# Moving sixteen checks of a matrix from one stage of a four-layer graph kernel to another

## The chip, the cores and the metric

The kernel runs on one core of a Trainium2 chip, in one launch. The metric is the device time of the launch in microseconds (us). Five engines have queues of their own: TensorE (PE, with its weight loads shown apart as PEld), VectorE (DVE), ScalarE (ACT), GpSimd (POOL) and SyncE (SP), the last of which here only issues transfers.

## The reference

Four layers of different graph networks share one node matrix `x` (4096 x 64) and one adjacency matrix `adj` (4096 x 4096, float32, entries 0 or 1). Each layer normalises `x`, computes its update and adds it.

```python
# layer 0: 8 attention heads over adj, then a second, single-headed attention on their output
mask = (adj > 0)[None]
...
e_o = jax.nn.leaky_relu(o1[:, None] + o2[None, :], ALPHA)
att_o = jax.nn.softmax(jnp.where(mask[0], e_o, NEG), axis=-1)
out = att_o @ Who
return jnp.tanh(out)
...
# layer 1: a weight and a distance for each pair of nodes
adj_att = jax.nn.sigmoid(left[:, None] + right[None, :] + b_att[0]) * adj
x_local = logmap(x[:, None, :], x[None, :, :], c)
support_t = jnp.einsum('ij,ijd->id', adj_att, x_local)
return proj(expmap(x, support_t, c), c)
...
# layer 2: mean of the neighbours, a dense layer, row norm
h_neigh = (adj @ X + X) / deg
...
# layer 3: the last 100 neighbours of a row, weighted by powers of one half
mask = (adj != 0).astype(support.dtype)
rank = jnp.cumsum(mask, axis=1)
...
w = mask * jnp.where(pos > 0, DECAY ** (k - pos), 0.0)
out = w @ support + bias
```

## The kernel before

The 4096 nodes are 32 blocks of 128 (`NB`), or 8 groups of 512 (`NG`). The adjacency matrix arrives transposed. It is turned once into bytes that are edge masks (0 or 56 as an integer, 0 or 1 as an 8-bit float) and written to DRAM as `mask_d`, one tile for each four blocks of sources (`q`, 8 of them) and half of the targets. All later stages read this mask and not the matrix.

That is only right if every value of the matrix is 0 or 1. So the kernel reads the whole float matrix a second time and checks it: `count_odd` (line 951) loads one 128 x 2048 piece (1 MB) into a tile `raw`, of which there are two, through SP's queue, and one DVE instruction (line 955) counts the elements for which "greater than 0" differs from the value itself. The count goes to one column of `bad`. There are 64 pieces; an iterator `todo` (line 959) hands out their numbers in order of the calls. At the end of the fast path (lines 2827 to 2830) the columns of `bad` are added on DVE, reduced over the partitions on GpSimd and compared with zero, and if anything was counted, the general kernel computes all again (line 2833). The calls of `count_odd` in the kernel before: sixteen in the output's attention (line 2105), and 48 beside the pairs of layer 1 (`check_edges`, line 2389).

The stages, one after another in the trace: the eight heads of layer 0 (to about 935 us), the output's attention with the node parts of layer 1 (to 1218), the pairs of layer 1 (to 1676), its closing and layer 2, and from about 1830 to 2030 the last layer.

*The output's attention* (lines 1957 to 2191). Four units `u` of 1024 targets each; a unit runs over eight blocks `q` of four source blocks. For each `q` SP loads a mask tile `mo` (three buffers); DVE makes its complement `nmo8`, which GpSimd's queue stores as `noedge_d` for layer 1; and for each pair of source blocks `split_edges` (line 1192) takes on ScalarE the sign of source score plus target score into `st` (line 1205), on DVE the products `B` (line 1211) and, for three pairs of four, `C` (line 1219). TensorE multiplies values with these products into `acco` (line 2132), and the factors of the denominators with `B` and `mo` into `ddo` (lines 2145, 2151). At a unit's end the sums are copied out (`evD`, `evB`, `evC`); `finish_unit` and the generator `layer1_nodes`, a long row of small DVE and ScalarE instructions, run within the next unit. The checks stand ahead of every other `q`. `behind(prepared.ins)` puts their DVE instruction behind the last one of the preparation.

*Layer 2 and the last layer* (`layers_fast`, line 2521). Layer 2 sums over the mask in two halves of the targets (tile `m`, line 2683) and closes each half with four calls of `layer2_group` (line 2628), each of which ends with the values of the last layer: `SS` and the remainder `lo` (line 2673). The last layer again has four units of 1024 targets and eight blocks `q` of mask tiles `m` (here called `m3`, line 2747, three buffers). For each of the 32 source blocks `j` TensorE computes the ranks into `pv` (lines 2754 and 2762), ScalarE turns them into weights `w` (`w3b`, line 2771), and TensorE adds the weighted values of the block before (`add_up`, line 2736) into two `sacc` banks. At a unit's end the sums are copied out to `ev` (line 2778), one by ScalarE and one by DVE, folded by TensorE (`pn3`), added to bias and `x` on DVE (`og`) and stored on GpSimd's queue (line 2793).

*Order.* The program is laid out by a scheduler that takes instructions by their place in the program as their inputs and buffers come free; each engine's queue then runs in that fixed order. A `with tc.issue_after(ins)` block adds one rule: instructions within it that run on the engine of `ins` come after `ins` there. Of a `count_odd` in such a block only the DVE instruction is bound if `ins` is on DVE; its load on SP's queue isn't. The pairs of layer 1 are in a block that keeps DVE, ScalarE and TensorE in the order of the program (`in_order`); the attention's units and the last layer are not.

Of the kernel before, what the change touches and what calls it, by code (L numbers as in the profile page):

```python
# [18 lines left out]
ALU = mybir.AluOpType  # L19
# [816 lines left out]
def kernel(  # L836
# [24 lines left out]
    nc = tc.nc  # L861
# [89 lines left out]
    def count_odd(pool, c):  # L951

        raw = pool.tile([P, HW], F32, name="raw", tag="raw", bufs=2)
        nc.sync.dma_start(raw, adjT[c % NB * P : (c % NB + 1) * P, c // NB * HW : (c // NB + 1) * HW])
        nc.vector.scalar_tensor_tensor(  # L955
            raw, raw, 0.0, raw, ALU.is_gt, ALU.not_equal, accum_out=bad[:, c : c + 1]
        )
# [83 lines left out]
    with ExitStack() as l0:  # L1041
# [134 lines left out]
        @contextmanager  # L1176
        def behind(*marks):

            with ExitStack() as e:
                for i in marks:  # L1180
                    e.enter_context(tc.issue_after(i))
                yield
# [726 lines left out]
        with ExitStack() as ob:  # L1909
# [185 lines left out]
            for u in range(4):  # L2095
                us = slice(u * HO2, (u + 1) * HO2)
                hs = slice((u % 2) * HO2, (u % 2 + 1) * HO2)
                accB, accC = (
                    [ps_acc.tile([P, G], F32, name="acco", tag="acc") for _ in range(NK)]
                    for _ in range(2)  # L2100
                )

                dd = ps_acc.tile([P, G], F32, name="ddo", tag="acc")
                for q in range(NQ):
                    if q % 2 == 0:
                        with behind(prepared.ins):
                            count_odd(work, next(todo))
                    m = work.tile([P, JT, HO2], U8, name="mo", tag="mo", bufs=3)
                    nc.sync.dma_start(m, mask_d[q][u // 2][:, :, hs])
                    nm8 = work.tile([P, JT, HO2], U8, name="nmo8", tag="nmo8")  # L2110
                    nc.vector.tensor_scalar(
                        nm8.bitcast(I32), m.bitcast(I32), EDGES4, None, ALU.bitwise_xor
                    )
                    nc.gpsimd.dma_start(noedge_d[q][u // 2][:, :, hs], nm8)
                    B2 = []
                    for t in range(0, JT, 2):
                        j0 = q * JT + t
                        edges = m[:, t : t + 2, :]
                        whole = j0 // 2 % 4 == 1
                        B, C = split_edges(  # L2120
                            work, srow[:, us], nto[:, j0 : j0 + 2], edges, j0, NB + 1, not whole, 4
                        )
                        B2.append(B)
                        products = [(accB, YB[:, j0 : j0 + 2], B), (accC, YC[:, j0 : j0 + 2], C)]
                        if whole:
                            products[1] = accC, YC[:, j0 : j0 + 2], edges.bitcast(F8)
                            yn = YCn[:, j0 // 8].rearrange("p i (s d) -> p i s d", d=D)
                            products.append((accC, yn, B))
                        for acc, Y, E in products:
                            for i in range(2):  # L2130
                                for k in range(NK):
                                    sums = nc.tensor.matmul(
                                        acc[k],
                                        lhsT=Y[:, i].rearrange("p s d -> p (s d)"),
                                        rhs=E[:, i, k * G : (k + 1) * G],
                                        start=j0 + i == 0,
                                        stop=acc is accB and j0 + i == NB - 1,
                                    )
                    with behind(sums.ins):
                        for t in range(JT):  # L2140
                            j = q * JT + t
                            fl = dict(start=(j == 0), stop=(j == NB - 1))
                            for k in range(NK):
                                ks = slice(k * G, (k + 1) * G)
                                nc.tensor.matmul(
                                    dd[k * O : (k + 1) * O, :],
                                    lhsT=YD1[:, j],
                                    rhs=B2[t // 2][:, t % 2, ks],
                                    **fl,
                                )  # L2150
                                nc.tensor.matmul(
                                    dd[(NK + k) * O : (NK + k + 1) * O, :],
                                    lhsT=YD2[:, j],
                                    rhs=m[:, t, ks].bitcast(F8),
                                    **fl,
                                )
                    if q == 0 and pending:
                        finish_unit(*pending)
                        beside = layer1_nodes(slice((u - 1) * OB, u * OB), work, aug)
                        pending = None  # L2160
                    elif u:
                        for _ in range(2):
                            next(beside, None)
                assert not u or next(beside, None) is None
                evD = work.tile([P, G], F32, name="evD", tag="evD", bufs=1)
                nc.vector.tensor_copy(evD, dd)
                em = work.tile([P, G], F16, name="emo", tag="emo", bufs=1)
                nc.vector.tensor_scalar(em, evD, 0.0, None, ALU.is_equal)
                evs = [evD]
                for k in range(NK):  # L2170
                    ev = work.tile([P, G], F32, name="evB", tag="evB", bufs=NK)
                    (nc.vector.tensor_copy if k else nc.scalar.copy)(ev, accB[k])
                    evs.append(ev)
                for k in range(NK):
                    nc.tensor.matmul(
                        accC[k],
                        lhsT=meano[NK * O :, k].rearrange("p s d -> p (s d)"),
                        rhs=em[NK * O :],
                        start=False,
                        stop=True,  # L2180
                    )
                    ev = work.tile([P, G], F32, name="evC", tag="evC", bufs=NK)
                    (nc.vector.tensor_copy if k else nc.scalar.copy)(ev, accC[k])
                    evs.append(ev)
                pending = (u, evs)
# [335 lines left out]
    def layers_fast(es, wide, *sums):  # L2521
# [41 lines left out]
            base=0,  # L2563
            channel_multiplier=1,
        )
        ready = []

# [58 lines left out]
        def layer2_group(b0, part, deg):  # L2628
# [41 lines left out]
                )  # L2670
            nc.scalar.copy(SS[:, bs, 0, :], pu)
            lo = work.tile([P, GB, D], F32, name="lo3", tag="lo3")
            nc.vector.tensor_tensor(lo, pu, SS[:, bs, 0, :], ALU.subtract)
            nc.scalar.activation(SS[:, bs, 1, :], lo, AF.Copy, scale=LO)


# [53 lines left out]
        for u in range(4):  # L2730
# [14 lines left out]
            for q in range(NQ):  # L2745
                m = work.tile([P, JT, HO2], U8, name="m3", tag="m3", bufs=3)
                nc.sync.dma_start(m, mask_d[q][u // 2][:, :, hs])
                for t in range(JT):
                    j = q * JT + t

                    pv = ps_v.tile([P, HO2], F32, name="pv", tag="pv")
                    for k in range(NK):
                        r = ((u % 2) * NK + k) * O
                        nc.tensor.matmul(  # L2754
                            pv[:, k * G : (k + 1) * G],
                            lhsT=blk[r : r + O, j, :],
                            rhs=late[r : r + O, u // 2, :],
                            start=True,
                            stop=False,
                        )  # L2760
                    for k in range(NK):
                        nc.tensor.matmul(  # L2762
                            pv[:, k * G : (k + 1) * G],
                            lhsT=tri,
                            rhs=m[:, t, k * G : (k + 1) * G].bitcast(F8),
                            start=False,
                            stop=True,
                        )

                    w = work.tile([P, HO2], I16, name="w3b", tag="w3b", bufs=3)  # L2770
                    nc.scalar.activation(w, pv, AF.Relu)  # L2771
                    if last is not None:
                        add_up(*last)
                    last = (j, w)
# [113 lines left out]
```

## Time and profile before

| what | value |
|---|---|
| median of 3 runs | 2041.64 us (2033.41 to 2043.93) |
| profiled execution | 2039.13 us |
| its span in the profile | 2037.1 us |
| granted TensorE clock over the span | 0.938 |
| PE busy | 1815.8 us (89%) |
| DVE busy | 1530.0 us (75%) |
| ACT busy | 1476.9 us (72%) |
| POOL busy | 83.3 us (4%) |
| one check on DVE (line 955), 64 of them | 2282 ns and 81 ns for its accumulator |
| its load, 1 MB, from issue to landing | 6.0 us (median) |

A table of windows gives, for stretches of the span, how long each engine was busy. A group line gives line, engine, operation, output and inputs, shapes and count, then after the bar the busy time, the mean of one in ns, and, after a second bar, how long the engine stood idle just before and what ended that. In a timeline line a bracket at the end says how long the engine had been idle and on whom it waited. TensorE's matmuls overlap each other, so the busy time of TensorE is an upper figure.

The page's slices (fortieths of the span, some 51 us each, digits are tenths) show the stages: DVE is busy to 7 to 9 tenths up to the 36th slice and idle in the last three, TensorE is busy nearly everywhere.

```profile
PE   5889989999999999996788958999999995789998
DVE  5779988998789879996989867888788788533000
ACT  2768987899689878993778847777777753227676
```

### The profile page before, as it was taken

The page shows a single profiled execution, that of the slowest core. Times are in us where ns is not written, and L with a number is a line of the kernel's source. Part 1 is how long each engine was busy: PE and PEld are TensorE (multiplying, and loading weights), DVE is VectorE, ACT ScalarE, POOL GpSimd, SP SyncE. Part 2 cuts the span into 40 slices and gives each one's busy share as a digit, 9 for nine tenths or more (in the row PEclk, how much of TensorE's full clock was granted, in tenths as well). Part 3 has the DMA queues.
Part 4 walks back from the last instruction along what each step waited for, and adds up shares of the span by engine and source line. Part 5 has one row for each costly group of instructions (what it writes and reads, how often), then busy time and mean ns, then how long its engine had stood idle before and what let it go on. Part 6 is the DMA issues. An engine that isn't in the chain of part 4 may idle for free. (4 is left out here: it accounts for less than half of the span.)

```text
span 2037.1 us, 44155 instructions
## 1 busy us (share of the span) xinstructions
PE 1815.8 (89%) x19323; PEld 821.8 (40%) x19340; DVE 1530.0 (75%) x2239; ACT 1476.9 (72%) x1439; POOL 83.3 (4%) x125
## 2 busy tenths in 40 slices
PE   5889989999999999996788958999999995789998
PEld 3444445444444444443234442333333333344332
DVE  5779988998789879996989867888788788533000
ACT  2768987899689878993778847777777753227676
POOL 2000100100000000001011100000000000000000
PEclk8899999999999999997899977999999996899999
DMA  9945555434211111103686406444344334412232
GB/s 112 178 115 99 100 99 72 164 118 172 86 49 49 48 49 54 54 2 125 254 276 227 163 17 235 137 145 143 124 140 140 124 134 151 152 63 70 91 99 64
DMA packets 117016, 239.05 MB, mean 117 GB/s; under 512 B 11062, under 2 KB 84006, under 8 KB 102054
## 3 DMA queue, kind: packets, MB, share of 16 engines
q1 hardware_dynamic: 101996, 192.95, 28.1%
q0 software_dynamic: 14816, 43.18, 11.8%
q8 instruction: 153, 2.51, 0.5%
q14 instruction: 51, 0.42, 0.1%
HBM read 245.37 MB, written 49.46 MB: 145 GB/s over the span
## 5 line engine op out<-in xcount | busy, mean ns | idle before, releaser
L1205 ACT ACTIVATE st<-srow,nt 128x2048 int8<-128x2048 f32 x352 | 682.8, 1994 | 78.9 <-DVE B L1211 78.1
L1211 DVE TENSOR_TENSOR B<-st,mres 128x1024 int32<-128x1024 int32 x256 | 311.7, 1220 | 70.5 <-PE accC L1541 46.6
L1541 PE MATMUL accB<-B,ybh 128*32 128x512 fp8e4 x3072 | 340.6, 384 | 13.3 <-DVE B L1211 13.3
L1541 PE MATMUL accD<-B,ybh 128*32 128x512 fp8e4 x2048 | 303.0, 388 | 23.0 <-DVE h L1657 23.0
L1541 PEld LDWEIGHTS <-ybh 128*32 128x32 bf16 (+1 forms) x6656 | 197.4, 98 | 236.8 <-issue 74.8
L1541 PE MATMUL accC<-mres,ych 128*32 128x512 fp8e4 x2272 | 269.2, 381 | 0.0
L1541 PE MATMUL accC<-B,ycn 128*32 128x512 fp8e4 x2272 | 269.0, 381 | 0.0
L1541 PE MATMUL accL<-B,ybh 128*32 128x512 fp8e4 x1536 | 221.6, 390 | 4.6 <-DVE h L1661 4.5
L1541 PEld LDWEIGHTS <-ych 128*32 128x32 f16 x4096 | 170.2, 99 | 116.1 <-issue 11.3
L1199 DVE TENSOR_SCALAR st<-srow,nt 128x2048 uint8<-128x2048 f32 x160 | 205.4, 1284 | 2.5
L2339 PE MATMUL accj<-sg,who 128*64 128x512 f32 (+1 forms) x512 | 197.8, 616 | 5.9 <-DVE sg L2332 5.5
L2339 PE MATMUL acci<-sg,who 128*64 128x512 f32 (+1 forms) x512 | 197.8, 616 | 0.0
L2295 ACT ACTIVATE yt<-pu,consts 128x512 f32<-128x512 f32 x144 | 98.7, 687 | 98.7 <-PE pu L2294 98.6
L2284 ACT ACTIVATE sg<-pl,rb 128x512 f32<-128x512 f32 x256 | 160.9, 679 | 8.2 <-PE pl L2279 5.2
L2771 ACT ACTIVATE w3b<-pv 128x1024 int16<-128x1024 f32 x128 | 131.0, 1024 | 42.4 <-PE pv L2762 41.2
L1205 ACT ACTIVATE st<-srowo,nto 128x1024 int8<-128x1024 f32 x128 | 138.3, 1138 | 25.0 <-DVE B L1211 24.9
L1541 PE MATMUL accC<-C,ych 128*32 128x512 fp8e4 x1824 | 149.3, 393 | 0.8 <-DVE C L1219 0.8
L955 DVE SCALAR_TENSOR_TENSOR raw<-raw 128x2048 f32<-128x2048 f32 x64 | 146.1, 2282 | 3.3 <-DMA raw<-in_adj_dram 3.3
L1219 DVE TENSOR_TENSOR C<-B,mres 128x1024 int32<-128x1024 int32 x114 | 139.5, 1225 | 3.6
L1541 PEld LDWEIGHTS <-ycn 128*32 128x32 f16 x2272 | 108.4, 97 | 62.7 <-issue 1.9
L2332 DVE SCALAR_TENSOR_TENSOR sg<-pf,sg 128x512 f32<-128x512 f32 x112 | 72.1, 685 | 38.9 <-PE pf L2329 38.9
L2778 DVE COPY ev<-sacc 128x512 f32<-128x512 f32 x4 | 2.8, 691 | 124.8 <-PE sacc L2736 124.8
(497 smaller groups left out, 2756.4 us busy)
## 6 DMA issues: line engine op xcount, KB each, us to landing
raw<-in_adj_dram SPq DMA_DIRECT2D x64, 1024.0 KB, 6.0
mo<-edges SPq DMA_DIRECT2D x32, 512.0 KB, 4.9
noedge<-nmo POOLq DMA_DIRECT2D x32, 512.0 KB, 4.3
nm<-noedge SPq DMA_DIRECT2D x64, 256.0 KB, 3.1
m<-edges SPq DMA_DIRECT2D x16, 1024.0 KB, 4.8
m<-edges SPq DMA_DIRECT2D x32, 512.0 KB, 3.8
srow<-srow_d SPq DMA_DIRECT2D x15, 1024.0 KB, 6.7
mres<-in_adj_dram POOLq DMA_DIRECT2D x8, 1024.0 KB, 35.4
```

Of the source, the lines that this page charges most:

```text
L955: nc.vector.scalar_tensor_tensor(raw, raw, 0.0, raw, ALU.is_gt, ALU.not_equal, accum_out=bad[:, c : c + 1])
L1199: nc.vector.tensor_scalar(st[:, i, :].bitcast(U8), srow, negs[:, i : i + 1], EDGE, ALU.is_gt, ALU.mult)
L1205: nc.scalar.activation(st[:, i, :], srow, AF.Sign, bias=negs[:, i : i + 1], scale=-1.0)
L1211: nc.vector.tensor_tensor(B.bitcast(I32), st.bitcast(I32), edges.bitcast(I32), ALU.bitwise_and)
L1219: nc.vector.tensor_tensor(C.bitcast(I32), B.bitcast(I32), edges.bitcast(I32), ALU.bitwise_xor)
L1541: ins = nc.tensor.matmul(acc[k * O : (k + 1) * O, :], lhsT=values, rhs=moving(k), start=start, stop=stop,)
L2284: nc.scalar.activation(sg[:, b0 + k, :], pl, AF.Sigmoid, bias=rb[:, j : j + 1], scale=1.0)
L2295: nc.scalar.activation(far[gi, gj][:, b, :], pu, AF.Sigmoid, bias=nb_t, scale=2.0 * DIST_K / (DIST_S * DIST_S),)
L2332: nc.vector.scalar_tensor_tensor(v[:, t, :], pf, F_K3, v[:, t, :], ALU.add, ALU.mult)
L2339: nc.tensor.matmul(acc[r : r + n, :], lhsT=XQ[:, src, cols], rhs=w, start=start, stop=stop)
L2771: nc.scalar.activation(w, pv, AF.Relu)
L2778: (nc.vector.tensor_copy if k % 2 else nc.scalar.copy)(ev[:, k, :], accs[k])
```

## The change

The sixteen calls leave the attention, and sixteen calls enter the last layer, at `j` = 4, 12, 20 and 28 of each unit, behind the ScalarE instruction that makes the weights. The last `lo` of `layer2_group` is the mark that their DVE instructions come after. As `todo` hands out numbers in order of the calls, the calls beside the pairs now take pieces 0 to 47 and those of the last layer 48 to 63. The `raw` tiles of the last layer come from the pool `work` of `layers_fast`.

```diff
@@ -2102,9 +2102,6 @@
                 for q in range(NQ):
-                    if q % 2 == 0:
-                        with behind(prepared.ins):
-                            count_odd(work, next(todo))
                     m = work.tile([P, JT, HO2], U8, name="mo", tag="mo", bufs=3)
                     nc.sync.dma_start(m, mask_d[q][u // 2][:, :, hs])
@@ -2563,7 +2560,7 @@
-        ready = []
+        ready, valued = [], []
@@ -2670,7 +2667,7 @@
             nc.scalar.copy(SS[:, bs, 0, :], pu)
             lo = work.tile([P, GB, D], F32, name="lo3", tag="lo3")
-            nc.vector.tensor_tensor(lo, pu, SS[:, bs, 0, :], ALU.subtract)
+            valued.append(nc.vector.tensor_tensor(lo, pu, SS[:, bs, 0, :], ALU.subtract))
             nc.scalar.activation(SS[:, bs, 1, :], lo, AF.Copy, scale=LO)
@@ -2769,6 +2766,9 @@
                     w = work.tile([P, HO2], I16, name="w3b", tag="w3b", bufs=3)
                     nc.scalar.activation(w, pv, AF.Relu)
+                    if j % 8 == 4:
+                        with tc.issue_after(valued[-1].ins):
+                            count_odd(work, next(todo))
                     if last is not None:
                         add_up(*last)
                     last = (j, w)
```

## The prediction

> **What bounds the kernel now.** I read the page first (engines by slice), then a table of windows by stage, then who waits for whom inside the two stages that the change touches, and last the rows of the moved instruction and of its neighbours in time. The chain of waits on the page is of little use here: it covers 18% of the span by engine and no line has over 1%. So I work by stage.
>
> The table of windows: for each stretch its length, then busy us (instructions) of TensorE, its weight loads, VectorE (DVE), ScalarE (ACT), GpSimd, then granted clock, DMA share, GB/s. The first four are the four units of the output's attention, cut where each unit's last `ddo` matmuls end; the last three are units 1 to 3 of the last layer.
>
> ```profile
> 973.10:1027.60 54.50, 45.91 (x280) 17.76 (x281) 50.20 (x72) 41.54 (x45) 4.99 (x7) 0.93 0.73 270
> 1027.60:1080.10 52.50, 46.16 (x311) 20.81 (x310) 46.94 (x110) 40.83 (x46) 5.70 (x8) 0.97 0.74 253
> 1080.10:1131.00 50.90, 45.16 (x297) 20.72 (x298) 47.43 (x109) 42.37 (x47) 5.69 (x8) 0.97 0.62 214
> 1131.00:1179.90 48.90, 46.65 (x334) 21.30 (x333) 37.17 (x98) 37.17 (x43) 4.99 (x7) 1.00 0.42 141
> ...
> 1894.00:1938.00 44.00, 43.40 (x204) 14.43 (x206) 2.21 (x5) 32.25 (x33) 1.55 (x2) 0.98 0.29 90
> 1938.00:1982.00 44.00, 43.45 (x207) 14.70 (x210) 2.21 (x5) 33.27 (x34) 1.50 (x2) 1.00 0.33 102
> 1982.00:2026.00 44.00, 42.97 (x202) 14.57 (x207) 2.21 (x5) 33.28 (x34) 1.49 (x2) 1.00 0.25 79
> ```
>
> In the attention DVE is busy 92%, 89%, 93% of units 0 to 2 and 76% of unit 3, where TensorE takes over (46.65 of 48.90). In the last layer TensorE is busy 98 to 99% and DVE 2.21 us of 44.
>
> Where the checks lie, by the windows of the tile `raw` alone (length, DVE busy and count, clock, DMA share, GB/s):
>
> ```profile
> 973.00:1031.50 58.50, 18.33 (x16) 0.93 0.74 269
> 1031.50:1083.50 52.00, 9.20 (x9) 0.97 0.74 254
> 1083.50:1133.00 49.50, 9.12 (x8) 0.97 0.58 202
> 1133.00:1182.00 49.00, 0.00 (x0) 1.00 0.42 140
> ```
>
> Each check is two records (compare and accumulator read), so eight checks run in unit 0, four in each of units 1 and 2, none in unit 3, although the program writes four per unit: they run as early as their loads allow. Unit 3 is thus a sample of a unit without checks, in the same trace.
>
> The attention's instruction groups (line, engine, operation, tiles, shapes, count | busy us, mean ns | idle before it, releaser), and then the waits:
>
> ```profile
> L955 DVE SCALAR_TENSOR_TENSOR raw<-raw 128x2048 f32<-128x2048 f32 x16 | 36.5, 2282 | 0.3 <-DMA raw<-in_adj_dram 0.3
> L1205 ACT ACTIVATE st<-srowo,nto 128x1024 int8<-128x1024 f32 x128 | 138.3, 1138 | 25.0 <-DVE B L1211 24.9
> L2132 PE MATMUL acco<-B,YBo 128*128 128x512 fp8e4 x256 | 69.7, 392 | 29.4 <-DVE B L1211 29.3
> ```
>
> ```profile
> 1068.41 1.75 PE L2132 MATMUL acco<-B,YBo 128*128 128x512 fp8e4 x6 [4.02 <-DVE B L1211]
> 1120.83 1.86 PE L2132 MATMUL acco<-B,YBo 128*128 128x512 fp8e4 x4 [4.46 <-DVE B L1211]
> 1169.52 1.02 PE L2132 MATMUL acco<-B,YBo 128*128 128x512 fp8e4 x4 [1.83 <-DVE B L1211]
> ```
>
> ACT and TensorE both wait for the DVE mask product `B`. The three rows of the timeline are one event in units 1, 2 and 3: the burst of small DVE operations of `layer1_nodes` holds `B` back. It costs TensorE 4.02 and 4.46 us where checks ran in the unit, and 1.83 where none did: DVE had not run ahead. After the long waits the matmuls are slow too (1.86 us for four against 1.02).
>
> **What the Trainium skill says.** *Perfetto Trace Analysis*, section "Optimization Strategy": a kernel whose most-contended engine changes over time may gain by interleaving its regimes; the two groups of windows are such regimes. *TensorE: Matmul & The Clock Gate*, section "Architectural detail: the array is 16× 32×32, not 1× 128×128": ACT and DVE queues are strict FIFO, so what stands behind a waiting check on DVE waits too. The trace agrees as far as it goes: a ScalarE copy of `accC` ran at 1083.76, the DVE copy of its sister only at 1085.67, when the check that began at 1083.46 was over. *DMA: Bandwidth & Descriptors*, section "Issuing engines are not separate DMA queues": transfers of all issuers interleave on the same 16 engines. The DMA share of 0.74 with checks against 0.42 without, in the rows above, fits.
>
> **The change part by part.**
>
> *Removed from the attention.* Sixteen compares of 2.282 us and sixteen accumulator reads of 0.08: 16 x 2.36 = 37.8 us of DVE, 16.8 MB of loads and 16 issues on SP's queue. This is not the gain, since TensorE is next. By unit:
> - Unit 0: DVE's 50.2 falls by 8 x 2.36 to 31.3. TensorE needs 4.54 and 5.4 us for the two kinds of mask block (blocks start with a group of `acco` matmuls at 1153.14, 1157.68 and 1163.08), so 4 x 9.94 = 39.8 us in a unit without closing work, and some 5 us of start (slow clock, 0.54 and 3.63 us of waits that are preparation, not checks). 45.5 in place of 54.5: -9. Two checks at 984.78 and 989.46 stand straight in the way there, as ACT is busy only 3.81 of the 10 us from 983. Bounds: -4.7 (those two alone) to -12.5 (42 us).
> - Units 1 and 2: TensorE is busy 46.16 and 45.16; idle 6.3 and 5.7 us. With unit 3's idle of 2.25 they give -4.1 and -3.5; I take -4 and -3. Bounds: 0 (the burst of `layer1_nodes` costs the same) to -5.5 and -5 (clock regained as well).
> - Unit 3: no checks; 0.
>
> Sum: -16, between -4.7 and -23. The stages behind start on what the attention ends with, so the gain is carried on whole.
>
> The loads of `mo` (SP) stand behind fewer transfers, and the `noedge` stores on GpSimd's queue come earlier; neither is on the path once TensorE binds, as `mo` buffers then come free with its own matmuls.
>
> *The 48 checks beside the pairs.* They now take columns 0 to 47 in place of 16 to 63: same count, size and slots. 0.
>
> *Added to the last layer, DVE.* The same 37.8 us over 4 x 44 us in which DVE has 2.21 us of work per unit: hidden. TensorE isn't slowed by a check beside it: with one running from 1073.93 to 1076.14 a group of four matmuls took 1.04 us, with none 1.03. Without that cover it would cost 37.8.
>
> *Added to the last layer, order on DVE.* All sixteen stand behind the last `lo3` (start 1890.70), so no group of layer 2 waits for a check. Behind a check stands the `ev` copy at each unit's end (1894.87, 1939.06, 1983.11, 2027.09), and behind it the next unit's accumulation, which has two `sacc` banks, and at the last unit the end. A check that is running delays it 2.36 at most; one whose load hasn't landed by 6.0 + 2.36 = 8.4. At four checks per 44 us the copy meets a running one with chance 0.21, mean rest 1.2 us: 1 us in all; I take +1.5. Bounds 0 to 4 x 8.4 = 33.
>
> *Added to SP's queue.* Sixteen issues of 0.33 us between the `m3` loads (3.8 us to landing). From the third on each waits for one of two `raw` slots, so an `m3` load behind it waits for a check. TensorE takes 4 x 1.375 = 5.5 us per `m3` tile and three are held, so 11 us of lead; slot and landing are 2.36 + 6.0, then 3.8: 12.2 at worst, some 1 us late in a bad case. Bounds 0 to 16 x 1.2 = 19; I take 0. The first two `raw` loads may go out at 1694, behind the three `m2` and three `m3` already sent, while the next `m2` isn't due before 1717: 0. The DMA share of 0.3 has room for 16.8 MB in 176 us (95 GB/s on top of 79 to 102; 383 were reached in the attention).
>
> *The flag behind the checks.* The sum of `bad` now runs at 1685.7, the all-reduce at 1689.1, the comparison at 1689.5, 340 us before the end. It now follows the last check, at latest j = 28 of unit 3, 4 x 1.375 = 5.5 us before the accumulation ends. Price 0.2 + 1.4 + 0.4 + 0.15 = 2.2, GpSimd's `out` stores and the engines' reads of the flag behind it. It ends before the last `og` unless the check is late: +0.5, bounds 0 to 4.
>
> Sum: -16 + 1.5 + 0.5 = -14 on the profiled execution's 2039.13 (span 2037.1 and 2.0 around it): 2025. The median shown, 2041.64, lies 2.5 higher; the three runs span 10 us. I give 2026, between the two scales.
>
> **The rivals.**
> - *Another wait takes its place* (0.16). `B` is late because of `layer1_nodes` and preparation, and the checks only filled time that was lost anyway. For: the 4 us waits coincide with the burst, with no check in the 4 us ahead. Against: 1.83 in unit 3. Then only the two early checks count: -4.7 + 2 = -3, 2037.
> - *More than the DVE time goes* (0.10). The clock (0.93, 0.97, 0.97 against 1.00) and the DMA share recover too, units at 42, 47, 46 us: -23 + 1, 2017. Against: part of the 0.93 is the start, which stays.
> - *Slower: the checks hold the `ev` copies* (0.13). If the order on DVE puts a check with an unlanded load ahead of each unit's copy, TensorE stands at each unit's end: 33 - 16 = +17, 2057. It decides from 4 us per unit end (16/4). For: two `sacc` banks, FIFO. Against: the loads can go out well before, with the SP queue mostly idle (checks waited 0.3 us for loads in the whole attention).
> - That nothing moves isn't possible: the lines are unconditional, and the DVE order in the last layer is forced behind `lo3`.
>
> **How the numbers follow.** Forecast 0.61, at 2026, own range 2018 to 2033. A measurement here tells no change from about 0.5%, 10 us: 2031.4 to 2051.9. Faster takes 0.57 of the forecast and the 0.10: 0.67; same 0.03 and 0.15: 0.18; slower 0.13 and 0.02 of further mishaps such as late `m3` loads: 0.15. The range, 2010 to 2044, takes in the gains down to -23 on either scale with some room and the rival without gain; it leaves out the slower side.
>
> **What would show it.** Right: the four attention units at about 45, 48, 48, 49 us with DVE under 80% and TensorE over 90%, the 4 us waits near 2; units of the last layer still at 44 with DVE near 12 us each; `ev` copies within 2 us of their `sacc`. Wrong: attention units still over 50; `sacc` or `pv` waiting on DVE or on `m`; the last check after 2020 and the flag's chain at the end.

## The result: 2022.6 us, and the profile after

Six runs of the changed kernel have a median of 2022.57 us (2017.45 to 2025.64), six of the kernel before, run beside them, 2040.91. The ratio is 0.9914, with an interval of 0.9896 to 0.9932: a gain of 17.6 us, between 14 and 21. A second group of runs gave 0.9925 (0.9903 to 0.9948). The forecast was 2026.

Where did it come from? The spans of the two first traces differ by 2037.1 - 2019.9 = 17.2 us. Three marks divide this: the last writing of `who`, with which the input of the output's attention is complete (955.25 before, 952.32 after), the cast of the first flag `again`, with which the nodes of layer 1 are done (1218.14 and 1200.66), and the end.

| stretch | before | after | difference |
|---|---|---|---|
| start to the last `who` | 955.25 | 952.32 | -2.9 |
| `who` to `again`: the output's attention | 262.89 | 248.34 | -14.55 |
| `again` to the end | 818.96 | 819.24 | +0.3 |

The first row isn't the change's. The first write to `bad`, far ahead of the change, came at 70.7 us before and at 67.1 after; in a second trace of each it came at 70.8 and 69.7, and in the traces of other kernels between 67.0 and 70.8. The start scatters by some 4 us. The second row is firmer: the second traces have 260.95 and 248.12, and three more kernels with the attention of the changed one have 246.2 to 248.9. The third row scatters by more than it shows: in the traces of the kernels below, but for the two that slow this stretch down, it is 814.5 to 824.4.

Now the attention by units, cut at the last writing of `who` and at each copy `evD`. First the kernel before, with the columns of the table of windows shown in the prediction (length, busy us of TensorE, weight loads, DVE, ACT and GpSimd, clock, DMA share, GB/s); here the first stretch includes the preparation.

```profile
955.25:1028.40 73.15, 46.64 (x281) 17.95 (x282) 68.04 (x122) 50.25 (x61) 11.28 (x13) 0.83 0.77 278
1028.40:1080.69 52.29, 46.42 (x312) 20.99 (x312) 46.73 (x109) 40.94 (x47) 5.70 (x8) 0.97 0.74 256
1080.69:1132.95 52.26, 46.52 (x315) 21.13 (x314) 48.32 (x110) 43.73 (x50) 5.91 (x9) 0.97 0.59 205
1132.95:1179.90 46.95, 44.70 (x314) 20.66 (x313) 35.69 (x96) 35.22 (x40) 4.76 (x7) 1.00 0.43 146
```

The same four windows of the changed kernel:

```profile
952.32:1023.02 70.70, 47.12 (x281) 18.19 (x282) 50.53 (x106) 50.51 (x62) 10.08 (x12) 0.78 0.40 130
1023.02:1069.32 46.30, 44.52 (x312) 20.46 (x312) 39.12 (x101) 39.66 (x45) 5.70 (x9) 1.00 0.54 182
1069.32:1116.11 46.79, 45.37 (x316) 20.85 (x315) 39.34 (x101) 42.51 (x48) 5.69 (x9) 1.00 0.55 180
1116.11:1162.20 46.09, 44.60 (x315) 20.57 (x313) 35.69 (x96) 35.82 (x41) 4.75 (x7) 1.00 0.43 149
```

Units 1 and 2 are now as short as unit 3, TensorE is busy 96 and 97% of them, and its clock is full. They gave 6.0 and 5.5 us, unit 3 gave 0.9. Unit 0 lost 17.5 us of DVE work and got only 2.45 us shorter: the row to explain.

The waits of TensorE in the attention of the changed kernel (who waits for whom, us in total, times, longest):

```profile
PE acco L2129 <- DVE fso L2007: 12.4, 1, 12.4
PE psso L2022 <- DVE wsum L2020: 8.5, 1, 8.5
PE acco L2129 <- DVE B L1211: 4.3, 4, 2.0
```

The same in the kernel before:

```profile
PE acco L2132 <- DVE B L1211: 29.3, 7, 17.0
PE psso L2022 <- DVE wsum L2020: 3.6, 1, 3.6
```

The 12.4 us are TensorE's idle time before the stage's first product, which stands before as the wait of 17.0 for `B`. Without it the waits for `B` fell from 12.3 to 4.3 us. The rows of the timeline around the second wait, and those of the burst of layer 1's node parts in units 1 to 3:

```profile
974.00 1.02 PE L2129 MATMUL acco<-B,YBo 128*128 128x512 fp8e4 x4 [2.00 <-DVE B L1211]
983.52 0.69 PE L2022 MATMUL psso<-wsum,ones 128*128 128x64 f32 x2 [8.50 <-DVE wsum L2020]
984.01 1.91 PE L2129 MATMUL acco<-B,YCn 128*128 128x512 fp8e4 x4
...
987.68 3.00 PE L2129 MATMUL acco<-C,YCo 128*128 128x512 fp8e4 x8
...
1057.87 1.02 PE L2129 MATMUL acco<-B,YBo 128*128 128x512 fp8e4 x4 [0.52 <-DVE B L1211]
...
1104.66 1.02 PE L2129 MATMUL acco<-B,YBo 128*128 128x512 fp8e4 x4 [0.60 <-DVE B L1211]
...
1151.82 1.02 PE L2129 MATMUL acco<-B,YBo 128*128 128x512 fp8e4 x4 [1.16 <-DVE B L1211]
```

The burst costs 0.52, 0.60 and 1.16 us in place of 4.02, 4.46 and 1.83: DVE has run ahead. But in unit 0 TensorE stands 8.5 us in front of `psso`, a pair of matmuls for the mean of the values that only the unit's end needs. It waits for a DVE sum of 3.97 us near the end of the preparation, and what stands behind it on TensorE waits too. *TensorE: Matmul & The Clock Gate*, section "The mechanism", says that matmuls start and end in the order of the program; the row at 987.68 agrees, as DVE had finished its two `C` by 975.9. `psso` alone is not the loss, though. The row at 984.01 reads `YCn`, which DVE made behind the same sum (983.38 to 983.80), so in this order TensorE would have stood nearly as long without `psso`.

So unit 0 falls into a part ahead of `psso` and one behind it. This is the part behind, from the start of `psso` to `evD`, before and after:

```profile
983.95:1028.40 44.45, 39.56 (x260) 15.50 (x261) 40.16 (x58) 31.36 (x31) 4.27 (x6) 0.96 0.88 323
983.52:1023.02 39.50, 39.34 (x256) 15.39 (x257) 22.71 (x41) 30.43 (x30) 4.54 (x7) 0.92 0.53 174
```

Behind `psso` TensorE now has no idle time to speak of (39.34 of 39.50), and that part gave 5.0 us. Ahead of it no check had stood: before, the first one began at 984.78. That part became longer, 31.2 us from the last `who` in place of 28.7, because DVE, in a new order, stood 2.7 us in front of results of ScalarE and GpSimd there, where it had stood in front of none.

The last layer, by windows between its `ev` copies, first all work and then the checks alone (length, DVE busy and count, clock, DMA share, GB/s):

```profile
1877.67:1921.82 44.15, 44.05 (x210) 14.69 (x208) 22.91 (x24) 32.25 (x33) 1.57 (x2) 1.00 0.89 322
1921.82:1965.57 43.75, 43.65 (x208) 14.55 (x206) 13.89 (x19) 33.00 (x34) 1.87 (x3) 1.00 0.60 202
1965.57:2009.80 44.23, 43.31 (x205) 14.45 (x204) 2.21 (x5) 33.24 (x34) 1.52 (x2) 1.00 0.24 76
```

```profile
1877.67:1921.82 44.15, 20.69 (x19) 1.00 0.89 322
1921.82:1965.57 43.75, 11.58 (x12) 1.00 0.60 202
1965.57:2009.80 44.23, 0.00 (x0) 1.00 0.24 76
```

Again the checks run as early as their loads allow and not four to a unit: two at the mark (1873.25 and 1875.46, in the last 5 us of unit 0), nine in unit 1, five in unit 2, none later. The units stay at 44 us although the DMA share reaches 0.89 in one. One copy `ev` per unit is on ScalarE and one on DVE; at the end of unit 1, where a check was in the way, they look so:

```profile
1921.29 0.58 ACT L2778 COPY ev<-sacc 128x512 f32<-128x512 f32 x1 [0.47 <-PE sacc L2733]
```

```profile
1919.61 2.29 DVE L955 SCALAR_TENSOR_TENSOR raw<-raw 128x2048 f32<-128x2048 f32 x1 [3.84 <-DMA raw<-in_adj_dram]
1921.82 0.08 DVE L955 DVE_READ_ACCUMULATOR raw<-raw 128x1 f32 x1
1921.82 0.69 DVE L2778 COPY ev<-sacc 128x512 f32<-128x512 f32 x1
```

DVE's copy came 0.53 us after ScalarE's. At the end of unit 0, right behind the two checks at the mark, it came 0.74 after (1.30 in the second trace). Where no check ran, the distance is 0.2 to 0.4. The flag behind the checks is ready 73 us before the end (by the tiles `odd` and `again`: count, duration, first and last start):

```profile
L2829 POOL PARTITION_ALL_REDUCE odd<-bad x1: 367/367/367, 1946.2 to 1946.2; - x1
L2830 DVE TENSOR_SCALAR again<-odd x1: 153/153/153, 1946.6 to 1946.6; 128x1 int32<-128x1 f32 x1
```

### The profile page after: what moved, and what is told of

Read it like the earlier page. It is cut to its first block, busy times and chain, and to the rows that moved or that the text cites. A ratio compares the mean times of both kernels' runs of the same rounds, so it can differ in the third digit from the quotient of the medians.

```text
span 2019.9 us, 44190 instructions
## 1 busy us (share of the span) xinstructions
PE 1810.5 (90%) x19340; PEld 818.8 (41%) x19340; DVE 1534.4 (76%) x2239; ACT 1474.5 (73%) x1439; POOL 83.4 (4%) x125
## 3 DMA queue, kind: packets, MB, share of 16 engines
q1 hardware_dynamic: 101996, 192.95, 28.4%
## 5 line engine op out<-in xcount | busy, mean ns | idle before, releaser
L2270 PE MATMUL pl<-nm,noid 128*128 128x512 fp8e4 x256 | 82.3, 393 | 13.8 <-ACT sg L2281 12.9
```

Of the source, the lines that this page charges most:

```text
L2270: nc.tensor.matmul(pl, lhsT=noid, rhs=nm[:, b, :].bitcast(F8), start=True, stop=False)
```

## The experiments

Two theories stood against each other at first. A: the gain is DVE time that left the attention, and the last layer hides what it got. B: it is the 16.8 MB of loads that left it. For each kernel the time of the stage from `who` to `again` is given beside the whole, since it isn't touched by the scatter of the start.

**The two kernels once more.**

> The changed kernel once more, for a second trace and a time beside the kernels of this group. Theory A (the gain is the DVE time that left the attention) and theory B (it is the 16.8 MB of loads that left it) both expect about 2022 us and a ratio of 0.991. In the first pair of traces 3.6 of the 17.2 us of difference were there at 70 us already, far ahead of the change: if that is chance of the start, the mark at which the first column of bad is written lies anywhere between 66 and 72 us here; if it belongs to the change, again near 67.

Measured 2023.11 us, ratio 0.9925; stage 248.1, units 71.1, 46.1, 46.9, 45.6 us. The first write to `bad` came at 69.7.

> The kernel before once more, for a second trace. If the breakdown by unit is the program's and not chance, the stage from the last copy of who to the cast of again is 262 to 264 us again (248.3 and 248.1 in the two traces of the changed kernel), and the units end 73, 125, 178 and 225 us after that copy; the first column of bad lies anywhere between 66 and 71 us.

One run of 2036.52 us; stage 260.95, units 73.5, 52.0, 52.2, 45.8. The stage is 1 us under what was expected. The breakdown by unit came out again in both kernels, unit 0 with a gain of 2.4 us and units 1 and 2 with 5.9 and 5.3.

**No checks in the last layer either.**

```diff
-                    if q % 2 == 0:
-                        with behind(prepared.ins):
-                            count_odd(work, next(todo))
...
-    todo = iter(range(2 * NB))
+    todo = iter(range(2 * NB - 16)); nc.gpsimd.memset(bad[:, 2 * NB - 16 : 2 * NB], 0.0)
```

> Leaves out sixteen of the 64 checks altogether (16.8 MB of the matrix aren't checked). Theory A, that the last layer hides its checks: the time of the changed kernel within 3 us, about 2021, and the units of the last layer at 44 us as there. If the checks cost something there (ev copies held, late mask tiles), this kernel is faster than the changed one by that: over 4 us.

2023.84 us, ratio 0.9931 (0.9903 to 0.9959); stage 248.7, distances of the last `ev` copies 43.88, 44.06, 44.24 us against 44.15, 43.75, 44.23 with checks. The times can't tell the cost of the moved checks from zero. The traces can: from the last `lo` to the last DVE copy `ev` it is 136.2 to 136.4 us in the seven traces of this record without checks in the last layer, and 136.5 to 136.9 in the six with the sixteen. Most of it is the first copy, which comes 4.75 us after that `lo` in place of 4.2, behind the two checks at the mark. So the moved checks cost half a microsecond, and that half of theory A holds.

**The loads alone, and the compares alone.**

```diff
-                            count_odd(work, next(todo))
+                            c = next(todo)
+                            raw = work.tile([P, HW], F32, name="raw", tag="raw", bufs=2)
+                            nc.sync.dma_start(raw, ...)
+                            nc.vector.tensor_scalar(bad[:, c : c + 1], raw[:, 0:1], 0.0, None, ALU.mult)
```

> The kernel before, with the sixteen loads left in the attention but in place of each compare one DVE instruction on a single column (leaves out sixteen of 64 checks). Theory A (DVE time): near the changed kernel, 2020 to 2027, ratio 0.990 to 0.993. Theory B (the loads are what mattered): near the kernel before, over 2035. Anything between splits the gain between the two.

2032.59 us, ratio 0.9971 (0.9957 to 0.9985): neither theory's value.

```diff
-                            count_odd(work, next(todo))
+                            c = next(todo)
+                            raw = work.tile([P, HW], F32, name="raw", tag="raw", bufs=2)
+                            spare = work.tile([P, 1], F32, name="spare", tag="spare", bufs=2)
+                            nc.vector.scalar_tensor_tensor(
+                                raw, srow[:, 0:HW], 0.0, srow[:, 0:HW], ALU.is_gt, ALU.not_equal,
+                                accum_out=spare,
+                            )
```

> The kernel before, with sixteen compares of the same size left in the attention, but on a tile that lies in SBUF anyway, and no loads (leaves out sixteen of 64 checks). Theory A: near the kernel before, 2034 to 2043, ratio 0.997 or more. Theory B: near the changed kernel, about 2023. Together with the kernel that keeps the loads alone it says whether the two add up.

2033.00 us, ratio 0.9979 (0.9966 to 0.9992): again between. The stages are 256.1 us with the loads and 255.8 with the compares, against 248.3 with neither and 261 to 263 with both. Each alone costs 7.5 to 8 us of the stage, and the two nearly add up there. Theory A as it stood falls, and B with it: taking either out of the kernel before gives 5 to 7 us. Units 1 and 2 of the kernel with the loads alone:

```profile
1025.60:1078.83 53.23, 47.72 (x313) 21.13 (x313) 39.92 (x108) 40.15 (x45) 5.93 (x9) 0.94 0.76 280
1078.83:1126.19 47.36, 45.46 (x314) 20.75 (x314) 39.67 (x102) 42.26 (x48) 5.71 (x9) 1.00 0.53 177
```

DVE has 39.92 us of work in unit 1, as without checks, and the unit is still 53.23 us long; in unit 2, where the loads have ended, it is 47.36. With the compares alone units 1 and 2 had 50.9 and 50.4 us; those compares, with no load to wait for, ran earlier than in the kernel before (the small write to `bad` that ends the preparation came 40.7 us after `who` in place of 34.1). By unit the two don't add up: against the changed kernel unit 1 lost 6.9 us with the loads alone and 4.6 with the compares alone, but 6.0 with both; unit 2 lost 0.6 and 3.6, but 5.5 with both. The loads alone ran earlier too, the last issued at 1049.0 in place of 1099.5. So both count, but a share of each unit for each of them isn't shown.

**Is it DVE's wait for the loads, or the traffic?** In the kernel with the loads DVE still stood 8.6 us in front of instructions whose `raw` hadn't landed. So the reader went to GpSimd.

```diff
-                        with behind(prepared.ins):
-                            count_odd(work, next(todo))
+                        c = next(todo)
+                        raw = work.tile([P, HW], F32, name="raw", tag="raw", bufs=2)
+                        nc.sync.dma_start(raw, ...)
+                        spare = work.tile([P, 1], F32, name="spare", tag="spare", bufs=2)
+                        nc.gpsimd.tensor_tensor(spare, raw[:, 0:1], YCn[:, 0, 0, 0:1], ALU.mult)
```

> The kernel before with the sixteen loads in the attention, no compares, and the loads read by one small GpSimd instruction each, so that DVE waits for no load of raw (leaves out sixteen of 64 checks). The loads alone with a DVE reader cost 7.5 us of the stage against none, and DVE waited 8.6 us for raw there. If that wait on DVE's queue was the cost, this kernel is at 2022 to 2026 and the stage (last copy of who to the cast of again) at 248 to 251 us. If the cost is the traffic itself (mask tiles mo late), it stays at 2030 to 2034 and 254 to 258 us.

2030.53 us, ratio 0.9946 (0.9918 to 0.9973), stage 252.7: between the two values again. Its first two units:

```profile
957.51:1030.69 73.18, 47.09 (x281) 18.16 (x282) 51.34 (x107) 51.23 (x62) 13.84 (x22) 0.80 0.76 284
1030.69:1080.36 49.67, 47.24 (x312) 20.92 (x312) 39.59 (x103) 40.15 (x46) 8.04 (x16) 0.93 0.83 306
```

Of the 7.8 us that the loads cost the stage, 3.4 go when DVE no longer waits for them (256.1 to 252.7); 4.4 stay with the traffic and with GpSimd's queue, at DMA shares of 0.76 and 0.83. This split rests on one trace of each, and equal attentions differ by up to 2.7 us. There the mask tiles `mo` took 4.7 us to landing in the median (5.0 with the reader on DVE) against 3.9 in the changed kernel, and DVE waited 23.9 us for them (20.4) against 17.7. That the late `mo` is the way in which the traffic costs isn't shown: in the kernel before `mo` took 4.9 us and DVE waited only 13.0 for it; GpSimd, too, stood 28.4 us in front of `raw`, with the `noedge` stores behind it; and in unit 1 of this kernel TensorE was hardly more idle than in the changed one (2.4 against 1.8 us) but busy 47.24 us in place of 44.52, with the clock at 0.65 in the unit's first 9.3 us.

**What the mark is worth.**

```diff
-                        with tc.issue_after(valued[-1].ins):
-                            count_odd(work, next(todo))
+                        count_odd(work, next(todo))
```

> The changed kernel without the mark: the checks of the last layer may run on DVE as soon as their loads land, in layer 2 too. Theory A: the first two loads land before 1690, so two checks run within layer 2, where DVE stands in the chain of each closing group, and each delays that chain by at most 2.4 us; later ones fall between the groups of the second half. 2023 to 2030, the last lo up to 5 us later against the start of layer 2. Rival: the mark is worth nothing as DVE has gaps of 3 to 5 us there: within 2 us of the changed kernel.

2051.61 us, ratio 1.0052 (1.003 to 1.0074): 29 us slower than with the mark, and slower than the kernel before. I had looked for the checks in layer 2's closing groups. They came far earlier, into the closing of layer 1. The stretch of 87 us from just before the first mask tile of layer 2, without and then with the mark:

```profile
1673.00:1760.00 87.00, 40.84 (x234) 19.99 (x234) 81.49 (x200) 22.95 (x37) 4.39 (x9) 0.66 0.83 299
```

```profile
1665.00:1752.00 87.00, 57.34 (x335) 28.38 (x335) 64.79 (x206) 26.98 (x45) 5.40 (x11) 0.74 0.51 177
```

DVE, which leads there through the rows of small steps that end layer 1, is full (81.49 of 87, 35 of them checks), TensorE does 40.84 us of work in place of 57.34, and the clock drops to 0.66. All sixteen checks were through by 1763. So the same 37.8 us cost half a microsecond behind the mark and, by the medians, 29 us without it.

**Twice the compares in the last layer.**

```diff
-                            count_odd(work, next(todo))
+                            raw = work.tile([P, HW], F32, name="raw", tag="raw", bufs=2)
+                            ...
+                            for into in (bad[:, c : c + 1], spare):
+                                nc.vector.scalar_tensor_tensor(
+                                    raw, raw, 0.0, raw, ALU.is_gt, ALU.not_equal, accum_out=into
+                                )
```

> The changed kernel with each of the sixteen compares of the last layer made twice (the second into a spare column): 37 us more on DVE there. Theory A, DVE is idle there: within 2 us of the changed kernel, 2021 to 2025, units of the last layer at 44 us. If the moved checks are near the point where they hold the ev copies: 4 us or more slower.

2029.22 us, ratio 0.9944 (0.9926 to 0.9963), 4 to 6 us slower than with one compare each by the ratios, though the intervals touch. The trace is clear: from the last `lo` to the last DVE copy `ev` it took 145.55 us in place of some 136.8. One row of the timeline shows most of it:

```profile
1927.09 1.97 PE L2792 MATMUL pn<-fold_3f,ev 128*128 128x64 f32 x8 [5.22 <-DVE ev L2787]
```

At the ends of units 0 and 1 the DVE copy `ev` stood behind compares and came 5.24 and 7.74 us after ScalarE's; at the second TensorE waited 5.22 us for it, and that unit took 48.1 us. This is the slower rival of the prediction, at two of four unit ends. The cover in the last layer isn't far from its end.

**Unit 0: the mean asked for later.** The block from `wsum` to `meano` became a function, called at `u == 0 and q == 4`.

```diff
+            def mean_parts():
+                wsum = spool.tile([P, D], F32, name="wsum")
+                ...
+                    if u == 0 and q == 4:
+                        with behind(prepared.ins):
+                            mean_parts()
```

> The changed kernel with one block of the preparation moved: the mean of the values (a DVE sum of 3.97 us, one matmul pair on TensorE, five small instructions), which only the end of the unit reads, is now asked for at block 4 of unit 0 and no longer ahead of it. It tests why unit 0 gained only 2.5 us of the 9 forecast. If TensorE stood 8.5 us behind the matmul that waits for that sum (its queue runs in order) and this is where the gain went, unit 0 gets shorter by 4 to 8 us and the time is 2015 to 2019. If unit 0 is held by the rest of the preparation on DVE, it stays within 2 us of the changed kernel.

2018.92 us, ratio 0.9889 (0.9866 to 0.9912); stage 244.1, unit 0 66.9 us. That is 3.8 us off unit 0, just under the expected band. With the sum no longer ahead of it on DVE, `YCn` was made 27.25 us after the last `who` in place of 31.06, the same 3.8 us earlier. So the sum's place on DVE accounts for the gain; that the place of `psso` on TensorE cost anything of its own isn't shown. TensorE stood in front of the late piece itself:

```profile
981.50 1.89 PE L2135 MATMUL acco<-B,YCn 128*128 128x512 fp8e4 x4 [5.02 <-DVE YCn L2044]
```

**The negated values in four parts**, on top of the late mean: each quarter of `YCn` right behind the quarter of `YC` that it negates.

```diff
+                def negated(g):
+                    return nc.vector.tensor_scalar(YCn[:, g], ..., -1.0, None, ALU.mult)
...
                 for g in range(1, 4):
                     staggered(parts(g, 0), parts(g, 1))
+                    prepared = negated(g)
```

> The kernel with the late mean, and the negated values YCn made in four parts, each as soon as its quarter of the values is there, in place of all at the end of the preparation. TensorE stood 5.0 us at the first product that reads YCn. If that wait was the next one on the path of unit 0: 3 to 5 us off unit 0, 2014 to 2016. If DVE's preparation holds the mask products behind it anyway: less than 2 us.

2016.84 us, ratio 0.9902 (0.9883 to 0.992); stage 239.6, unit 0 62.6 us, 4.3 less. So with the mean late `YCn` was the input that held this unit.

> The kernel with the late mean and the early negation once more, since its interval overlaps that of the changed kernel although its stage was 8.7 us shorter in the trace (239.6 against 248.3). If the gain of the stage is carried to the end, the ratio to the kernel before lies at 0.988 to 0.990 again and the stage at 239 to 241 us; if the later stages give it back, at 0.991 to 0.993.

2016.54 us, ratio 0.987 (0.9838 to 0.9901); stage 241.2, unit 0 62.95. The two medians lie some 6 us under the two of the changed kernel (2022.57, 2023.11), while the stage is 7 to 9 us shorter. This version beats the kernel before clearly; against the changed kernel the intervals of the ratios still overlap, and it is the stage that shows the difference.

**More buffers**, on top of the late mean: `mo` in five tiles, `B` in six.

> The kernel with the late mean, and in the attention five mask tiles mo in place of three and six products B in place of four, so that DVE may run further ahead of TensorE before the burst of layer 1's node parts. If the waits of TensorE for B (4.2 us in the stage) and of DVE for mo (17 us) still cost something, 2 to 4 us faster than with the late mean alone: about 2015. If TensorE binds units 1 to 3 so that nothing waits behind it, the same within 2 us, about 2019.

2020.53 us, ratio 0.9919 (0.99 to 0.9938), stage 246.4: no gain. The first product started later (971.03 against 967.11), so the order had shifted as well; the test says only that these buffers aren't a simple gain.

## Why the prediction was right, and where not

- *The bound and the direction.* Right. In units 1 to 3 TensorE took over at 46 to 47 us with its clock at 1.00, and the burst's waits fell under 2 us.
- *The sum for the attention, -16.* Measured -14.55, -12.8 in the second traces. Its terms were mis-sized against each other. Unit 0, forecast at -9, gave -2.45; units 1 and 2, forecast at -4 and -3, gave -6.0 and -5.5; unit 3, forecast at 0, gave -0.9 (-0.2 in the second traces). Too much in one and too little in the others cancelled; that the sum came so near is in part luck.
- *Unit 0* failed in the step "TensorE needs 39.8 us and some 5 us of start". The prediction's own line for this unit has TensorE busy 45.91 us, and the two waits that I kept as preparation are 4.17 us more; these make 50.1 and not 45.5, a gain of 4.4 in place of 9. The part behind `psso` gave 5.0. The part ahead of it, which I took as fixed, grew by 2.5: TensorE began its first product 4.5 us sooner and put four more matmuls ahead of `psso`, but DVE waited there, and TensorE's wait rose from 3.6 to 8.5 us. Behind that stood `YCn`, late by the same sum on DVE. I didn't ask what is late next when the checks are gone. Two experiments took another 8 us off this unit, but by changing the preparation itself, which the prediction didn't do; what they would give in the kernel before wasn't tried.
- *Units 1 and 2*: the mechanism was right and the size too small. TensorE's idle time fell by 4.1 and 4.3 us (5.87 to 1.78 and 5.74 to 1.42), near the 4.1 and 3.5 of the sum. The rest, 1.9 and 1.15 us, is TensorE's own busy time (46.42 to 44.52 and 46.52 to 45.37), at a clock of 1.00 in place of 0.97. The prediction had the regained clock in its bounds and at nothing in its sum. It also gave the loads that leave no price in the attention; alone they cost the stage 7.8 us.
- *The last layer, +1.5 for the held copies and +0.5 for the flag.* Measured some +0.5 for the copies, most of it at the end of unit 0, where the two checks at the mark stood; at the end of unit 1 a copy next to a check was 0.53 us behind ScalarE's. For the flag nothing can be told: the last check ended at 1945.8, 74 us before the end and not at its place in the program, and what follows the last addition of `x` scatters from 7.1 to 8.5 us with and without the checks. My picture of four checks in each unit was wrong here, although the same trace had shown them running early in the attention.
- *The mark.* That all sixteen stand behind the last `lo3` I used only to exclude a delay in layer 2. It carries more: without it the change loses.
- *The rivals.* "Another wait takes its place" came true in unit 0 alone, with a wait that I had listed, `psso`, growing from 3.6 to 8.5 us. "The checks hold the `ev` copies" cost half a microsecond at sixteen compares and nearly 9 us, at two unit ends, at thirty-two.

## What to carry to other kernels

Work that is moved out of a saturated stage can give back its transfer as well as its instruction, and only down to the next wait of the engine that takes over; look for that wait in the order of the engine that feeds it, where a long instruction that is needed late (here a sum of 3.97 us) can stand ahead of an input that is needed now. In the stage that receives it, the work is free only behind a mark that keeps it out of the stage ahead: the same checks cost half a microsecond or 29 us by that one rule. When two terms of a sum are estimates, compare them by unit afterwards, since a right total can hide two wrong ones.

## What the runs showed that I had not expected

The start of the program scatters: the same early instruction falls anywhere from 67.0 to 70.8 us, and the last `who` from 952.3 to 957.8 in kernels that hardly differ up to there, so a difference of spans below some 5 us says little until it is cut at marks. Cut finely enough, two traces can show half a microsecond: from the last `lo` to the last `ev` copy, kernels with equal work there agree within 0.4. Sixteen loads of 1 MB beside 512 KB mask tiles, at a DMA share of 0.76 to 0.83, cost the stage 4.4 us in one trace even when GpSimd alone read them. And the granted clock of TensorE went with the length of a unit: in units 1 and 2 it was 0.93 to 0.97 where they took 49.7 to 53.2 us, and 0.97 to 1.00 where they took 46.1 to 48.6.
